# A perceiver block on one core: span attention's last steps placed in another half batch, and the order within a stretch reversed

## The chip, the cores and the metric

The kernel runs on one core of a Trainium2 chip. The metric is the device time of one execution in microseconds. Of the kernel before there are three unprofiled runs, 1526.94 us (the median), 1526.82 and 1529.74, and one profiled execution whose trace is read here.

## What is computed

Three residual blocks follow one another on `x` (32 batches x 64 positions x 256): cross attention to a context of 1601 keys per batch, "span" attention among the 64 positions, and a feed-forward part with one shared expert and 8 experts chosen by a hash of the token's position, two for each. All in float32, 16 heads of 16.

```python
x = x + cross_attention(layernorm(x), ctx, mask)        # q, k, v, softmax over 1601 keys, out
# span attention, h = layernorm(x):
span = head_reshape(h @ W_span.T, 2); value = head_reshape(h @ W_val.T, D)
mean = sigmoid(span[..., 0]) * m;     soft = softplus(span[..., 1])
diff = pos[None, None, :] - mean[..., None]
attn = softmax(-soft[..., None] * (diff * diff), axis=-1)
x = x + (attn @ value).reshape(b, m, hs) @ W_out.T
# feed-forward, xf = layernorm(x):
shared = silu(xf @ sw1 + sb1) * (xf @ sw3 + sb3) @ sw2 + sb2
x = x + (shared + sum_of_two_experts(xf) / 2) / 2
```

## The kernel before, in words

**Cross attention: 64 half batches of three stretches.** The context comes in transposed, and its 1601 keys are cut into 13 chunks of 124. A half batch `n` is a batch `b = n // 2` and one half `c` of the heads. The loop at L765 goes over the half batches, software pipelined: while the softmax of half batch `n` runs, TensorE computes the scores of `n + 1` (`psc` and `pvs`, L548), the product with the values for `n - 1` (`pvs`, L635) and the projections of the next batch's keys and values (`pk`, `pv`, L494). The softmax's maximum takes a round trip: running maxima on VectorE (`mrun`, `mx`, L589), transposes on TensorE (`pm`, L596), a reduction on VectorE (`mc`, L603), transposes back (`pb`, L611), a copy by ScalarE (`mb`, L615). Then GpSimd subtracts the maxima (L620, four instructions per half batch) and ScalarE takes the exponentials (L625). Each half batch has three stretches, numbered `3n + g`; between the cross attention's own pieces each calls `run(stretch)`, once.

**Everything else is placed by an agenda.** `agenda[stretch]` is a list of generators. `run(stretch)` advances each generator of the list up to its next `yield`; the yielded number says how many stretches later it goes on. Three kinds of generators go through it: `query_steps(t)` (the next tile's layer norm, the transposes `tr_q`, the query product `pq` and its four copies into `qbd`, L465 to L480), `finish_steps(b)` (L704: divides a batch's attention output by its sums and transposes it into `oT`) and `span_steps(t)` (L244), which holds the output product of cross attention and the whole span attention of a tile.

**A tile is two batches, so four half batches are a period.** The 16 tiles' span attentions are cut into 23 steps each, and four tables tell the stretch of each step, counted from the tile's start: `STEPS` for tiles 0 to 12, `LAST_BUT_TWO`, `LAST_BUT_ONE` and `LAST` for tiles 13, 14 and 15. Counted from zero, the steps that matter here are:

| step | what it does | lines |
|---|---|---|
| 0 | output product `po` of cross attention, residual, layer-norm statistics | L250, L253, L197-199 |
| 1, 2 | spread on GpSimd, normalisation `xn_h` on ScalarE | L205-208, L214 |
| 3 | transposes `tr_h`, copy to `hT` (ScalarE) | L221, L262 |
| 4, 5, 6 | `psp` and its copies, exponential `z`, 17 small VectorE operations | L266-305 |
| 7, 8, 9 | scores `sc` on GpSimd, ScalarE (square) and GpSimd again; `least` on VectorE | L310-318 |
| 10-13 | 16 exponentials with their sums, four per step, ScalarE | L322 |
| 14-16 | value product `pval`; reciprocal `total`; product on GpSimd | L334-348 |
| 17, 18 | transposes `psa`, copies `aT`; product `po2`, copy `o2T` | L356-372 |
| 19 | second output product `po3` (shown as `po<-woutT_sb,o2T`), residual, statistics, store of `x_kept` | L376-381 |
| 20, 21 | spread on GpSimd, normalisation `xn_f` on ScalarE | L205-214 |
| 22 | transposes `tr_f`, two copies into `xfT` (ScalarE) | L221, L389 |

In the tables a value `v` of tile `t` stands for stretch `3n + v` of half batch `n = 4t + 4`; so 24 is the first stretch of half batch `4t + 12`, 30 that of `4t + 14`. Half batches are spoken of by `n mod 4`: the "third" of a period is the one with 2.

**What sets the order.** TensorE, VectorE, ScalarE and GpSimd execute in the order in which the code issues (L731). SP, which issues the DMAs, is ordered by the tile scheduler. PSUM banks for products come from one rotating set (`mm_bank`), so an early reader of a bank can be what a later product waits for.

**The end.** After the loop, the last half batch is finished, and the stretches from 2 to 21 after it are run by L849 on. There `unit(u)` is one of 16 pieces of the shared expert (two products of `xfT` with `sw1` and `sw3`, four matmuls, `u`, L664), and `gate()` its SiLU on ScalarE (L686, L691) and product on VectorE (L687, L692). `begin` says after which stretch which units start and `gated` how many gates follow. Units 12 to 15 need the last tile's `xfT`, and after them come the experts (L900 to L941).

Of the kernel before, what the change touches and what calls it, by code (L numbers as in the profile page):

```python
# [89 lines left out]
def perceiver_kernel(ctx: ExitStack, tc: tile.TileContext, a: dict[str, bass.AP], out: bass.AP):  # L90
# [126 lines left out]
    def transposed(src, name: str):  # L217
# [10 lines left out]

    STEPS = (3, 4, 5, 6, 7, 8, 9, 11, 12, 15, 16, 17, 18, 19, 20, 20, 21, 22, 23, 24, 25, 26, 27)
    LAST_BUT_TWO = (
        3, 4, 5, 6, 7, 8, 9, 11, 12, 13, 13, 14, 15, 16, 17, 17, 17, 18, 20, 21, 22, 25, 27,
    )
    LAST_BUT_ONE = (
        2, 2, 3, 4, 5, 5, 6, 7, 8, 9, 10, 11, 12, 13, 14, 14, 14, 15, 16, 17, 17, 18, 19,
    )
    LAST = (2, 2, 3, 4, 5, 6, 8, 9, 10, 11, 12, 12, 12, 12, 13, 13, 13, 15, 16, 17, 17, 18, 19)
    SMALL = 6
# [1 line left out]
    def steps_of(t: int):  # L241
        return (STEPS, LAST_BUT_TWO, LAST_BUT_ONE, LAST)[max(0, t - NTILE + 4)]

# [339 lines left out]
    def maximum(n: int, k: int):  # L583

        dst = mrun
        if k == NKC - 1:
            dst = mxs[n] = work.tile([P, 4, P], F32, tag="mx", bufs=1, name="mx")
        dst, run = (m[:CHUNK].rearrange("p (r i) q -> p r i q", r=2) for m in (dst, mrun))
        nc.vector.tensor_tensor(dst, block_of(n, k), run, ALU.max)  # L589
# [105 lines left out]
    held_at: set = set()  # L695

    def run(stretch: int):
        for steps in agenda.pop(stretch, []):
            while (wait := next(steps, None)) == 0:
                pass  # L700
            if wait:
                agenda[stretch + wait].append(steps)
# [62 lines left out]
    for n, (b, c) in enumerate(halves[:-1]):  # L765
# [9 lines left out]
        def steps(g: int):  # L775
            run(3 * n + g)
            for u in extra.get(3 * n + g, ()):
                linear_factor(u)
# [14 lines left out]
        if not held:  # L793
            first_maxima(n + 1)
        run(3 * n)
        if n:
            values(n - 1, 1)
# [30 lines left out]
    stretch = 3 * last  # L828
# [17 lines left out]
    gate()  # L846


    begin = {4: (1, 2), 7: (7, 8, 5), 10: (9,), 12: (10,), 15: (6, 4), 19: (11,)}  # L849
    gated = {7: 2, 10: 2, 12: 1, 13: 1, 15: 1, 17: 2}  # L850
    for s in range(2, 22):
        run(stretch + s)
# [149 lines left out]
```

## Time and profile before

| | us |
|---|---|
| median of three runs (lowest, highest) | 1526.94 (1526.82, 1529.74) |
| the profiled execution | 1529.89 |
| its span, first to last instruction | 1528.1 |
| `pm` of half batch 63, where the end begins | 1362.03 |
| mean granted TensorE clock | 0.996 of full speed |

The page counts for each engine the time in which an instruction of it was under way; an engine can be busy for most of the span and still not be what the end waits for. The timeline gives groups of like instructions in the order of their start; a bracket behind a row says how long the engine had been idle before it, and what ended this. Times in the timeline are microseconds from the span's start. "PEld" is TensorE's loading of weights, which overlaps its matmuls. DMA moves 46 GB/s over the span in the mean, and the transfers of the context come ahead of their use.

### The profile page before, as it was taken

Reading aid. Unit: us, or ns where it says so; the run is one execution under the profiler, and the core shown is the slowest. Engines: PE = TensorE matmul, PEld = TensorE weight load, DVE = VectorE, ACT = ScalarE, POOL = GpSimd, SP = SyncE. Lnnn points to the kernel's source line nnn. Section 1 sums busy time; section 2 is a strip of 40 time slices with the busy share of each in tenths; the row PEclk is TensorE's granted clock in tenths of the full one; section 3 lists DMA queues with packets and bytes.
Section 4 is the critical chain, followed back from the end, with each engine's and each line's share of the span. In section 5 each row is a group of like instructions: output and inputs, shape, how many; then the busy total and the mean of one; then the engine's idle time right before and its main releaser. Section 6 shows DMA issues by size and latency. Waiting matters only on the chain.

```text
span 1528.1 us, 62953 instructions
## 1 busy us (share of the span) xinstructions
PE 1470.4 (96%) x28600; PEld 1071.4 (70%) x28600; DVE 1222.8 (80%) x2332; ACT 947.7 (62%) x1727; POOL 1119.0 (73%) x508
## 2 busy tenths in 40 slices
PE   8999999999999999999999999999999999988999
PEld 5677767777777767777776767676777767654587
DVE  4889898988889898989888898888898889873100
ACT  3565657676667657676767666675767676756411
POOL 1777787888878887879878788878788787852610
PEclk9999999999999999999999999999999999999999
DMA  5111111111111101111111111111111111004100
GB/s 173 43 38 46 46 46 46 44 45 49 49 49 50 42 23 46 53 36 49 49 50 49 50 49 32 33 45 53 36 50 49 50 46 32 6 6 159 59 28 29
DMA packets 52076, 73.82 MB, mean 48 GB/s; under 512 B 3812, under 2 KB 51040, under 8 KB 51680
## 3 DMA queue, kind: packets, MB, share of 16 engines
q1 hardware_dynamic: 50992, 69.00, 14.7%
q8 instruction: 225, 3.69, 1.0%
q10 hardware_dynamic: 816, 0.79, 0.2%
q14 instruction: 43, 0.35, 0.1%
HBM read 65.57 MB, written 4.19 MB: 46 GB/s over the span
## 4 chain that ended last, share of the span: by engine, by line
PE 72%; DVE 17%; ACT 8%; issue 2%; POOL 0%; DMA 0%; ACTq 0%; DVEq 0%; POOLq 0%
PE pv L494 18%; PE pk L494 18%; PE psc L548 11%; PE pvs L635 8%; DVE mrun L589 7%; DVE prob L572 6%; PE py L932 4%; ACT sc L322 3%; PE pm L596 2%; ACT prob L625 2%; PE u L664 2%; PE ph L914 2%; PE pb L611 2%; PE pq L465 1%; PE psa L356 1%
## 5 line engine op out<-in xcount | busy, mean ns | idle before, releaser
L620 POOL TENSOR_TENSOR prob<-prob,mb 124x1664 f32<-124x1664 f32 x252 | 937.7, 3745 | 239.4 <-ACT mb L615 231.6
L572 DVE TENSOR_TENSOR prob<-psc,madd 124x512 f32<-124x512 f32 x768 | 506.6, 680 | 70.8 <-PE psc L548 69.2
L625 ACT ACTIVATE prob<-prob 124x1664 f32<-124x1664 f32 x256 | 406.9, 1590 | 181.7 <-POOL prob L620 179.1
L589 DVE TENSOR_TENSOR mrun<-prob,mrun 124x512 f32<-124x512 f32 x704 | 486.1, 691 | 40.7 <-ACT mrun L581 28.0
L494 PE MATMUL pk<-ct,wkT_sb 128*32 128x372 f32 (+1 forms) x2512 | 387.6, 489 | 5.7 <-DMA wkT_sb<-in_wkT 5.6
L494 PE MATMUL pv<-wvT_sb,ct 128*124 128x256 f32 x3524 | 380.9, 379 | 0.4 <-DVE prob L572 0.3
L494 PEld LDWEIGHTS pv<-wvT_sb,ct 128*124 128x124 f32 x3524 | 273.6, 132 | 108.7 <-issue 14.9
L548 PE MATMUL psc<-qbd,kT 32*124 32x128 f32 x6400 | 246.6, 280 | 17.0 <-ACT hT L262 9.7
L494 PEld LDWEIGHTS pk<-ct,wkT_sb 128*32 128x32 f32 (+1 forms) x2512 | 148.9, 127 | 135.9 <-issue 88.9
L548 PEld LDWEIGHTS psc<-qbd,kT 32*124 32x124 f32 x6400 | 204.7, 182 | 54.7 <-issue 19.7
L526 ACT COPY v<-pv 124x512 f32<-124x512 f32 (+1 forms) x224 | 124.4, 556 | 164.0 <-PE pv L494 163.9
L635 PE MATMUL pvs<-prob,v 124*17 124x64 f32 x13312 | 214.3, 220 | 1.2 <-issue 1.2
L635 PEld LDWEIGHTS pvs<-prob,v 124*17 124x17 f32 x13312 | 196.7, 98 | 23.1 <-issue 15.2
L509 ACT ACTIVATE kT<-pk,cols 128x372 f32<-128x372 f32 (+2 forms) x256 | 146.7, 585 | 69.1 <-PE pk L494 69.0
L322 ACT ACTIVATE sc<-sc,least 128x64 f32<-128x64 f32 x256 | 85.7, 339 | 2.8 <-DVE least L318 2.8
L934 DVE SCALAR_TENSOR_TENSOR ot<-py,prob 128x256 f32<-128x256 f32 x16 | 6.8, 424 | 75.7 <-PE py L932 75.7
L581 ACT COPY mrun<-prob 124x512 f32<-124x512 f32 x64 | 38.2, 597 | 41.4 <-DVE soft L305 38.3
L664 PE MATMUL u<-xfT,sw_sb 128*128 128x512 f32 x128 | 61.1, 627 | 0.9 <-ACT xfT L389 0.9
L596 PE MATMUL pm<-cst,mx 124*128 124x124 f32 x256 | 42.1, 285 | 17.0 <-DVE mx L589 14.1
L611 PEld LDWEIGHTS pb<-cst,mc 128*124 128x124 f32 x256 | 29.5, 135 | 36.8 <-DVE mc L603 28.9
L548 PE MATMUL pvs<-qbd,kT 32*124 32x128 f32 x256 | 54.9, 294 | 0.0
L565 DVE TENSOR_TENSOR prob<-psc,madd_fifth 124x256 f32<-124x256 f32 x64 | 27.0, 421 | 32.2 <-PE pvs L548 31.1
(126 smaller groups left out, 1242.4 us busy)
## 6 DMA issues: line engine op xcount, KB each, us to landing
ct<-in_ctxT SPq DMA_DIRECT2D x64, 372.0 KB, 3.2
ct<-in_ctxT SPq DMA_DIRECT2D x32, 496.0 KB, 5.1
ct<-in_ctxT SPq DMA_DIRECT2D x32, 361.0 KB, 4.0
w<-in_w SPq DMA_DIRECT2D x16, 256.0 KB, 7.0
x<-in_x SPq DMA_DIRECT2D x16, 128.0 KB, 2.1
x_kept<-x SPq DMA_DIRECT2D x16, 128.0 KB, 1.8
prob<-x_kept SPq DMA_DIRECT2D x8, 256.0 KB, 5.6
out<-ot SPq DMA_DIRECT2D x16, 128.0 KB, 1.9
```

The lines of the kernel that those rows point to most:

```text
L322: nc.scalar.activation(sc[:, h, :], sc[:, h, :], AF.Exp, bias=least[:, h : h + 1], scale=-1.0, accum_out=total[:, h : h + 1],)
L494: nc.tensor.matmul(out[at:end], lhsT=lhsT[:, at:end], rhs=rhs, start=start, stop=stop, **(dict(tile_position=(0, at)) if tiled else {}),)
L509: nc.scalar.activation(kTs[c][:, k0 : k0 + kn], ps[:, :kn], AF.Identity, bias=cols[:, B_K + c : B_K + c + 1])
L526: nc.scalar.copy(vs[b % 2][:kn, 2 * u : 2 * u + n, :, :DK], ps[:kn, : n * D].rearrange("p (n h d) -> p n h d", n=n, d=DK),)
L548: product = nc.tensor.matmul(ps[:CHUNK, at * P : (at + 1) * P], lhsT=kTs[c][32 * j : 32 * j + 32, k0 : k0 + CHUNK], rhs=qbd[b // 2][32 * j ...
L572: nc.vector.tensor_tensor(pair_of(n, j)[:, c0 : c0 + 4, :].rearrange("p k (e q) -> p k e q", e=2), pss[j][:CHUNK].rearrange("p (k e q) -> ...
L589: nc.vector.tensor_tensor(dst, block_of(n, k), run, ALU.max)
L596: nc.tensor.transpose(ps[:, j * CHUNK : (j + 1) * CHUNK], m[:CHUNK, j, :], ident[:CHUNK, :CHUNK])
L620: engine.tensor_tensor(sj, sj, m[:CHUNK, j, None, :].to_broadcast([CHUNK, NKC, P]), ALU.subtract)
L625: nc.scalar.activation(pair_of(n, j), pair_of(n, j), AF.Exp)
L635: nc.tensor.matmul(pvs[32 * j : 32 * j + DK + 1, c, :, r, :], lhsT=v[:kn, k, 8 * c + h, :], rhs=pair_of(n, h // 2)[:kn, k, (h % 2) * S : ( ...
L664: nc.tensor.matmul(ps, lhsT=w[:, c, hc * P : (hc + 1) * P], rhs=xfT[:, c, :, slot], start=(c == 0), stop=(c == 1),)
```

## The change

It has four parts. In `STEPS` the last four steps go from 24 to 27 to 30 to 33, that is from the half batches with 0 and 1 (mod 4) to those with 2 and 3. In `LAST_BUT_TWO` and `LAST_BUT_ONE` late steps are taken to earlier stretches: tile 13's last four from 21, 22, 25, 27 to 21, 21, 21, 23 with the one ahead of them unchanged at 20; tile 14's sixteen exponentials are all in one stretch, and what follows them is two stretches earlier. `run` goes through its list from the back, so of the generators in a stretch the one that was put into it last is advanced first. And units 1 and 2 begin one stretch earlier. No operation is added or removed.

```diff
-    STEPS = (3, 4, 5, 6, 7, 8, 9, 11, 12, 15, 16, 17, 18, 19, 20, 20, 21, 22, 23, 24, 25, 26, 27)
+    STEPS = (3, 4, 5, 6, 7, 8, 9, 11, 12, 15, 16, 17, 18, 19, 20, 20, 21, 22, 23, 30, 31, 32, 33)
     LAST_BUT_TWO = (
-        3, 4, 5, 6, 7, 8, 9, 11, 12, 13, 13, 14, 15, 16, 17, 17, 17, 18, 20, 21, 22, 25, 27,
+        3, 4, 5, 6, 7, 8, 9, 11, 12, 13, 13, 14, 15, 16, 17, 17, 17, 18, 20, 21, 21, 21, 23,
     )
     LAST_BUT_ONE = (
-        2, 2, 3, 4, 5, 5, 6, 7, 8, 9, 10, 11, 12, 13, 14, 14, 14, 15, 16, 17, 17, 18, 19,
+        2, 2, 3, 4, 5, 5, 6, 7, 8, 9, 10, 10, 10, 10, 12, 12, 12, 13, 14, 15, 15, 16, 17,
     )
...
     def run(stretch: int):
-        for steps in agenda.pop(stretch, []):
+        for steps in reversed(agenda.pop(stretch, [])):
             while (wait := next(steps, None)) == 0:
                 pass
...
-    begin = {4: (1, 2), 7: (7, 8, 5), 10: (9,), 12: (10,), 15: (6, 4), 19: (11,)}
+    begin = {3: (1, 2), 7: (7, 8, 5), 10: (9,), 12: (10,), 15: (6, 4), 19: (11,)}
```

## The prediction

> **What bounds the kernel now.** I read the page first: engine totals, then the chain that ended last.
>
> ```profile
> span 1528.1 us, 62953 instructions
> PE 1470.4 (96%) x28600; PEld 1071.4 (70%) x28600; DVE 1222.8 (80%) x2332; ACT 947.7 (62%) x1727; POOL 1119.0 (73%) x508
> ...
> PE 72%; DVE 17%; ACT 8%; issue 2%; POOL 0%; DMA 0%; ACTq 0%; DVEq 0%; POOLq 0%
> ```
>
> TensorE has work for 1470.4 of 1528.1 us, so some 58 us of idle is all that a reordering can win. I then listed TensorE's waits (columns: engine, line waited for; total us, times, longest):
>
> ```profile
> PE pm L596 <- DVE mx L589: 14.1, 16, 2.4
> ...
> PEld psc L548 <- ACT hT L262: 11.8, 11, 1.1
> ...
> PE psc L548 <- ACT hT L262: 9.7, 11, 0.9
> ```
>
> Two waits recur about once for each of the tiles. The second is one event seen twice, by weight loads and by matmuls. To place them I cut one period (a tile, four half batches) at the pm transposes (L596) and asked for each engine's busy time per stretch: bounds and length, then PE, PEld, DVE, ACT, POOL busy with counts, the granted clock, DMA share, GB/s. The first row is half batch 8, the others 32 to 35.
>
> ```profile
> 198.43:217.69 19.26, 18.45 (x409) 13.30 (x409) 17.52 (x32) 10.82 (x14) 16.20 (x6) 1.00 0.04 13
> 704.96:725.12 20.16, 19.35 (x416) 13.93 (x413) 18.68 (x35) 12.48 (x15) 17.90 (x9) 1.00 0.06 20
> 725.12:745.48 20.36, 20.36 (x431) 14.77 (x431) 18.84 (x33) 13.33 (x28) 17.09 (x11) 1.00 0.24 70
> 745.48:768.05 22.57, 21.70 (x461) 16.48 (x457) 18.17 (x34) 18.21 (x47) 16.82 (x6) 1.00 0.06 20
> 768.05:788.64 20.59, 20.59 (x469) 15.22 (x465) 18.89 (x42) 12.58 (x18) 17.01 (x6) 1.00 0.25 71
> ```
>
> I call the four classes 0 to 3 (n mod 4). Classes 1 and 3 have no TensorE idle: what is added there is paid in full. Class 0 idles 0.81, class 2 0.87 (plus late weight loads). The timeline names both (start, length, what; in brackets the idle before it and who ended it):
>
> ```profile
> 725.12 0.64 PE L596 MATMUL pm<-cst,mx 124*128 124x124 f32 x4 [0.81 <-DVE mx L589]
> 751.91 0.82 PE L548 MATMUL psc<-qbd,kT 32*124 32x128 f32 x20 [0.87 <-ACT hT L262]
> 751.50 0.36 ACT L262 COPY hT<-tr_h 128x256 f32<-128x256 f32 x1
> 707.55 1.03 PE L376 MATMUL po<-woutT_sb,o2T 128*128 128x256 f32 x4
> ```
>
> Class 2: scores cannot start until ScalarE has copied hT out of a bank (end 751.86), and ScalarE runs without a gap from 743.34 to 752.12. The last row is po3 in class 0.
>
> **The change, part by part.** TensorE's and VectorE's instruction counts stay the same; places change.
>
> *Class 0 loses po3, the residual and statistics.* po3 starts at 707.55, the next work at 708.51: a slot of 0.96. Half batch 8 does all of this class but po3 and lasts 19.26 against 20.16: **−0.90**, with the 0.81 wait in both. So the VectorE chain that ends in mx moves with TensorE rather than standing still: it runs without a gap from 711.51 and starts on TensorE's scores. I take −0.89, for 13 tiles.
>
> *Class 1 loses tr_f (0.44) and its two copies.* Half batch 9, without tr_f, lasts 20.17 against 20.36: **−0.20**, 13 times. The reversal also puts x += po before the reduction of least; it may wait 0.2 for TensorE, and VectorE's mx is 1.06 ahead of pm there.
>
> *Class 2 gains po3 (0.87 where banks are free), residual 0.42, statistics 0.43 and 0.18.* po3 goes ahead of the values, so TensorE reaches the scores later; hT's end, which releases them, is ScalarE's and doesn't move. The scores begin 4.86 after pm (750.34), their first dozen, whose banks are free, takes some 0.4; so with po3 ahead the one that waits is reached at 4.86 + 0.87 + 0.4 = 6.1, and hT ends at 6.38. Hidden, with 0.3 to spare (issue stops before the last matmul ends, so the listed 0.87 is short of the true stall). VectorE's added 1.03 lies in its 1.57 of idle ahead of mrun. If that cover goes, po3 costs its 0.87, and the scores are late next. At stretch 1 the reversal puts pq and the qbd copies ahead of psp and z; pq's bank goes to the second pk, which comes to wait for the 1.48 of qbd: pq would end 758.93, copies 760.48, pk due 760.31: **+0.2**. Bounds: 0 (pk still later) and 1.1 (pq's whole length); I stay with the nearest row.
>
> *Class 3 gains spread, norm and tr_f with xfT following in the next class.* GpSimd idles 6.3 ahead of its next mask work there, so the 1.28 of spread is hidden; the transposes are not: **+0.22** (the mirror of class 1), 12 times; the thirteenth is in the end.
>
> *SP's queue.* The x_kept store moves with the residual, behind the first context load of the odd batch instead of the even one; the next x load behind it is wanted some three half batches later. 0; if that cover went, x's 2.1 us landing would show once per tile.
>
> *The reversal at the heavy stretch.* A generator is requeued as it ran, so a reversed list flips at every stretch. In the built order class 2, stretch 0, still has the four exponentials ahead of hT: the 0.87 stall keeps its cause. Half batches 6 and 10 meet the flip without the removal: +0.2 each.
>
> Loop: 13 × (−0.89 − 0.20) = −14.2; 12 × (0.2 + 0.22) = +5.0; half batch 62's po3, which meets no stall, +0.87; first two +0.4. Sum **−7.9 us**. Unnamed 1 to 1.9 us stalls of TensorE ("issue", eight of them) may fall differently: ±3.
>
> *The end* (pm of 63 at 1362.03, the span's end at 1528.1). Here tile 15's own chain decides:
>
> ```profile
> 1379.33 1.10 PE L250 MATMUL po<-woP_sb,oT 128*128 128x256 f32 x4 [1.59 <-DVE oT L718]
> ...
> 1385.83 0.44 PE L221 MATMUL tr_h<-cst,xn_h 128*128 128x128 f32 x2 [0.58 <-ACT xn_h L214]
> 1387.61 1.09 PE L356 MATMUL psa<-cst,sc 128*128 128x128 f32 x8 [1.34 <-POOL sc L348]
> 1388.54 0.54 PE L266 MATMUL psp<-wspanT_sb,hT 128*128 128x32 f32 x4
> ...
> 1390.02 9.98 PE L664 MATMUL u<-xfT,sw_sb 128*128 128x512 f32 x20
> 1399.84 1.03 PE L376 MATMUL po<-woutT_sb,o2T 128*128 128x256 f32 x4
> 1404.02 0.44 PE L221 MATMUL tr_f<-cst,xn_f 128*128 128x128 f32 x2 [3.15 <-ACT xn_f L214]
> ```
>
> In the changed order tile 14's psa stands ahead of tile 15's po in TensorE's queue; psa waits for tile 14's exponentials, total and GpSimd's 1.90 product. These stay where they are (psa about 1387.5 against 1387.61), so po(15) goes from 1379.33 to 1388.4: +9.1. Behind it: x at 1389.5 (1380.47), xn_h +6.8, psp 1394.8 (1388.54), units 7, 8, 5 from 1395.35, +5.3. Tile 15's small VectorE work follows +5.9. Part is absorbed: before, ScalarE was held by table load and gates until the square at
>
> ```profile
> 1407.39 1.05 ACT L314 ACTIVATE sc<-sc 128x1024 f32<-128x1024 f32 x1
> ```
>
> and after it is free; the square starts 1411.4, +4.0. From there the chain (mult, least, exponentials, product, psa, po3, tr_f, last units, experts) is the same as before. So +4.0, and up to +5.5. Bounds: +9.1 (nothing absorbed) and −3 (the 3.15 wait for xn_f goes and nothing takes its place).
>
> *Two rules of the Trainium skill.* "TensorE: Matmul & The Clock Gate", section "Part 1: The HAM clock gate", speaks against: about 3.4 us of little work halves TensorE's clock, for about 3.4 us. In this trace the granted clock was 0.50 from 1388.9 to 1392.3, after waits of 0.58 and 1.34, and four matmuls of a unit took 2.96 instead of 1.72. In the changed end TensorE would idle about 4 us ahead of psa(15). By the rule that is an additional 1.7 us, by the row 1.24. As before has one such window already and the phase is unknown, I count 0.3: end **+4.3**. "ScalarE: Activation LUTs", "What ACT_TABLE_LOAD costs", gives 2.66 us per switch with its drain. The change orders the exponentials together and saves two of eight loads in the end: −5.3 by the rule. The trace has 1.28 for one (1376.86 to 1378.14, with the instruction before it ending at 1376.84: no drain), so −2.6, and the chain passes by TensorE and VectorE there: counted 0.
>
> Sum: −7.9 + 4.3 = **−3.6**. The profiled run took 1529.89 (span 1528.1), so 1526.3 on its terms; it lies 2.95 above the median 1526.94, from which the forecast is **1523.4**.
>
> **Rivals.** A measurement here tells 0.2%, 3.05 us, from no change.
> - *Slower: po3 isn't hidden in class 2.* The hT copy, or the bank before it, moves with TensorE, so the stall comes after po3 in its full length. For: in class 0 a chain did move with TensorE, the spare is only 0.3, and VectorE's mrun or a bank may come late instead. Against: what ScalarE's run up to hT takes from TensorE (pb, tr_h) is queued ahead of po3. Price 12 × 0.87 = 10.4: 1533.8. From 0.56 per period up the kernel is slower by over 0.2%.
> - *The end doesn't slip*: units fill psa's wait, xn_f's 3.15 goes. −7.9 − 3: 1516.0. Against: po(15) really stands behind psa(14).
> - *The class 0 wait grows by what po3 frees* (mx doesn't move): loop −7.9 + about 4, the end +4.3: 1527.3. Half batch 8 speaks against it.
>
> **Chances.** Forecast 0.48 (its own range 1520.5 to 1526.5: ±3 of issue stalls; 0.30 of it under 1523.9, 0.18 within 0.2%); slower rival 0.24; end that doesn't slip 0.18; cancelled 0.10. Faster 0.48, same 0.28, slower 0.24. The range 1516 to 1532 leaves out about half of either outer rival, some 0.2.
>
> **What would show it.** Right: class 0 near 19.3, class 1 near 20.15, class 2 near 22.75 with hT's stall no longer among the waits, class 3 near 20.8; po(15) 27 us after pm of half batch 63 instead of 17; six table loads in the end. Wrong: class 2 above 23.2; pm waiting over 1.5 in class 0; or units 7, 8, 5 starting within 2 us of their former place.

## The result: slower, though undisturbed half batches came out as worked

The changed kernel takes 1537.37 us (median of four runs, 1535.69 to 1538.26) against 1527.78 us (four runs, 1526.82 to 1529.74): the ratio is 1.006, with a 95% interval of 1.0042 to 1.0077. The profiled execution took 1537.91 us. Its page gives these totals:

```profile
span 1535.9 us, 62938 instructions
...
PE 1476.5 (96%) x28600; PEld 1072.8 (70%) x28600; DVE 1223.3 (80%) x2332; ACT 944.7 (62%) x1725; POOL 1119.9 (73%) x508
```

TensorE has as many instructions as before (28600 matmuls) but is busy for 6.1 us more: the same instructions took longer. The page alone does not say where. The same cut as in the prediction, at the pm transposes, for half batches 48 to 51 (bounds and length, then busy time of PE, PEld, DVE, ACT, POOL with counts, granted clock, DMA share, GB/s):

```profile
1042.53:1061.82 19.29, 18.48 (x409) 13.33 (x409) 16.56 (x30) 10.42 (x13) 15.71 (x5) 1.00 0.01 4
1061.82:1081.96 20.14, 20.14 (x429) 14.43 (x429) 18.85 (x33) 13.05 (x24) 16.86 (x11) 1.00 0.23 64
1081.96:1104.67 22.71, 22.38 (x465) 17.01 (x461) 19.07 (x37) 18.32 (x48) 17.71 (x9) 1.00 0.08 26
1104.67:1125.48 20.81, 20.81 (x471) 15.44 (x467) 18.89 (x42) 13.62 (x21) 17.23 (x6) 1.00 0.27 81
```

These are the lengths that recur in each class: 19.29, 20.14, 22.71 and 20.81 us. The forecast had 19.3, 20.15, 22.75 and 20.8. Per period that is some 0.73 us less than before, over the twelve periods from half batch 12 to 59 8.7 us. But not every half batch has its class's length: in class 3 only three of the twelve do, and their mean is 21.68 us (before: seven of twelve at 20.59, mean 21.02). Besides, pm of half batch 63 stands at 1361.06, a mere 0.97 us earlier than before (1362.03). From there to the end of the span it takes 174.80 us instead of 166.08. So two places have to be explained: nearly 10 us that the loop gave back, and 8.7 us lost in the end.

**The loop: half batches that are longer than their class.** TensorE's waits (engine, line waited for; total us, times, longest) have this row in the kernel before:

```profile
PE psc L548 <- issue: 5.6, 8, 1.6
```

And these in the changed kernel:

```profile
PE pm L596 <- DVE mx L589: 14.3, 17, 2.4
PE psc L548 <- issue: 8.4, 11, 1.6
...
PE psc L548 <- ACT hT L262: 2.7, 11, 0.9
```

The hT wait has fallen from 9.7 to 2.7 us, though it still occurs 11 times where the forecast had it gone; mx's is what it was. The row between them is the one to look at: "issue" means that TensorE waited for nothing that the profile shows. Half batch 19 has the longest, here in TensorE's timeline (start, length, what; in brackets the idle time before it):

```profile
446.17 0.81 PE L548 MATMUL psc<-qbd,kT 32*124 32x128 f32 x17
448.58 0.71 PE L548 MATMUL psc<-qbd,kT 32*124 32x128 f32 x15 [1.60 <-issue]
449.22 0.64 PE L596 MATMUL pm<-cst,mx 124*128 124x124 f32 x4
449.70 3.10 PE L494 MATMUL pk<-ct,wkT_sb 128*128 128x496 f32 x4
```

The scores stop in the middle of a group of 32 like matmuls. The DMA view of 443 to 449.5 us (queue, packets, MB, share of 16 engines) shows what else went on:

```profile
q1 hardware_dynamic: 816, 1.26, 62.5%
q8 instruction: 1, 0.02, 0.8%
```

Three pieces of context fill the DMA engines, and one packet of instructions goes in their midst. The trace's packet records put this packet at 446.18 to 447.06; TensorE resumes at 448.58, 1.5 us after. Of the unnamed stalls of over 0.6 us in half batches 12 to 59 of both kernels, each one resumes 1.2 to 1.6 us after such a packet has ended. TensorE's instructions themselves place the stalls further. Counting the matmuls and weight loads in the trace, before's six such stalls come after 12411, 17502, 21064, 36843, 38624 and 42187 of them, with 48, 68, 82, 144, 151 and 165 packets fetched: 254.4 to 254.6 instructions for each packet between neighbours. The changed kernel's nine give 254.4 to 254.8. So these stalls all lie at the same place, the end of a fetched block. A second thing is in the last row above: four pk matmuls took 3.10 us where they take 1.83 elsewhere. The granted clock says why (same columns as above):

```profile
450.10:453.50 3.40, 3.40 (x8) 1.55 (x6) 2.24 (x4) 0.66 (x1) 0.00 (x0) 0.50 0.00 0
453.50:456.90 3.40, 3.40 (x147) 2.97 (x147) 1.70 (x3) 2.08 (x4) 2.49 (x1) 0.99 0.02 5
```

After the stall the clock was 0.50 for 3.4 us, and half batch 20 became 1.69 us longer than its class. Adding up what half batches 12 to 59 are longer than the recurring length of their class gives 8.2 us in the kernel before and 17.9 in the changed one. I call this sum "stalls" below; in half batch 20 it includes the slow clock. Of it, 5.1 us before and 10.4 in the changed kernel lie in class 3, 2.0 and 5.8 in class 0.

**The end.** TensorE's timeline of the changed kernel from the last half batch on (tile 14's psa, then po(15), the po of tile 15; the last four rows are tile 15's psa, po2 and po3 and the last tr_f):

```profile
1382.73 1.98 PE L664 MATMUL u<-xfT,sw_sb 128*128 128x512 f32 x4 [2.20 <-ACT prob L691]
1386.32 1.09 PE L356 MATMUL psa<-cst,sc 128*128 128x128 f32 x8 [1.61 <-POOL sc L348]
1387.25 1.03 PE L250 MATMUL po<-woP_sb,oT 128*128 128x256 f32 x4
...
1391.69 1.61 PE L376 MATMUL po<-woutT_sb,o2T 128*128 128x256 f32 x4 [2.82 <-ACT o2T L372]
1393.09 0.63 PE L221 MATMUL tr_h<-cst,xn_h 128*128 128x128 f32 x2
1394.19 1.06 PE L266 MATMUL psp<-wspanT_sb,hT 128*128 128x32 f32 x4 [0.46 <-ACT hT L262]
1395.06 10.79 PE L664 MATMUL u<-xfT,sw_sb 128*128 128x512 f32 x20
...
1423.83 1.97 PE L356 MATMUL psa<-cst,sc 128*128 128x128 f32 x8 [3.63 <-POOL sc L348]
1425.73 1.40 PE L366 MATMUL po<-aT,vbd 128*32 128x64 f32 x32
1427.91 2.08 PE L376 MATMUL po<-woutT_sb,o2T 128*128 128x256 f32 x4 [0.79 <-ACT o2T L372]
...
1434.90 0.38 PE L221 MATMUL tr_f<-cst,xn_f 128*128 128x128 f32 x2
```

Of these last rows, the kernel before has:

```profile
1419.50 1.09 PE L356 MATMUL psa<-cst,sc 128*128 128x128 f32 x8 [1.05 <-POOL sc L348]
...
1422.76 1.13 PE L376 MATMUL po<-woutT_sb,o2T 128*128 128x256 f32 x4 [1.01 <-ACT o2T L372]
...
1427.16 0.38 PE L221 MATMUL tr_f<-cst,xn_f 128*128 128x128 f32 x2
```

po(15) starts 26.2 us after pm of 63 (17.3 before), psp 33.1 (26.5), the square (step 8) of tile 15 50.7 (45.4). At psa(15) the kernel is 5.3 us behind, and from there on the same instructions are slower: psa 1.97 instead of 1.09, po3 2.08 instead of 1.13. The clock over two stretches:

```profile
1392.20:1399.00 6.80, 6.34 (x14) 3.50 (x13) 2.70 (x7) 2.10 (x4) 1.03 (x3) 0.50 0.54 173
1422.90:1433.10 10.20, 8.39 (x48) 5.26 (x49) 3.07 (x6) 4.38 (x8) 2.57 (x6) 0.50 0.04 13
```

That is 17.0 us at half clock, where the kernel before has 6.8, in two windows (both have another 6.8 where the end begins):

```profile
1388.90:1392.30 3.40, 3.40 (x37) 2.07 (x37) 0.38 (x2) 2.59 (x4) 0.00 (x0) 0.50 1.10 349
1406.00:1409.40 3.40, 3.40 (x6) 1.29 (x5) 1.78 (x3) 3.39 (x6) 0.88 (x1) 0.50 0.02 5
```

When the last transposes tr_f are reached, the 5.3 us have become 8.7.

### The profile page after: what moved, and what is told of

It reads as the page before. It is cut to its first block, busy times and chain, and to the rows that moved or that the text cites. A ratio compares the mean times of both kernels' runs of the same rounds, so it can differ in the third digit from the quotient of the medians.

```text
span 1535.9 us, 62938 instructions
## 1 busy us (share of the span) xinstructions
PE 1476.5 (96%) x28600; PEld 1072.8 (70%) x28600; DVE 1223.3 (80%) x2332; ACT 944.7 (62%) x1725; POOL 1119.9 (73%) x508
## 4 chain that ended last, share of the span: by engine, by line
PE 70%; DVE 17%; ACT 8%; issue 2%; POOL 1%; DMA 1%; POOLq 0%; DVEq 0%; SPq 0%; ACTq 0%
PE pk L494 18%; PE pv L494 18%; PE psc L548 10%; PE pvs L635 9%; DVE mrun L589 7%; DVE prob L572 6%; PE py L932 4%; PE u L664 2%; ACT sc L322 2%; PE pm L596 2%; ACT prob L625 2%; PE ph L914 2%; PE pb L611 2%; ACT qbd L473 1%; PE pq L465 1%
## 5 line engine op out<-in xcount | busy, mean ns | idle before, releaser
L596 PE MATMUL pm<-cst,mx 124*128 124x124 f32 x256 | 41.5, 283 | 15.5 <-DVE mx L589 14.3
```

The lines of the kernel that those rows point to most:

```text
L596: nc.tensor.transpose(ps[:, j * CHUNK : (j + 1) * CHUNK], m[:CHUNK, j, :], ident[:CHUNK, :CHUNK])
```

## The experiments

The "end" in the table is from pm of half batch 63 to the end of the span; it, pm and the stalls come from the one profiled execution of each run, the ratio from the timed runs against the kernel before on the same chip. The runs are spread over several chips.

| run | ratio (95% interval) | pm of 63 | stalls | end |
|---|---|---|---|---|
| before | | 1362.0 | 8.2 | 166.1 |
| changed | 1.006 (1.0042-1.0077) | 1361.1 | 17.9 | 174.8 |
| before, no loads | 0.9964 (0.9952-0.9976) | 1357.7 | 4.9 | 166.2 |
| changed, no loads | 0.999 (0.9981-0.9999) | 1352.3 | 9.3 | 174.6 |
| end tables alone | 0.9995 (0.9986-1.0005) | 1365.0 | 11.1 | 163.6 |
| STEPS alone | 0.9951 (0.9935-0.9968) | 1355.3 | 13.4 | 165.9 |
| reversal alone | 1.0025 (1.0016-1.0034) | 1365.7 | 11.0 | 167.5 |
| STEPS and reversal | 1.0003 (0.9992-1.0013) | 1365.3 | 21.2 | 168.3 |
| all but the reversal | 0.9937 (0.9917-0.9957) | 1354.7 | 11.8 | 162.5 |
| all, reversal in the loop only | 0.9995 (0.9987-1.0003) | 1362.7 | 18.7 | 164.2 |

### Without context loads

Theory A: the stalls are instruction fetches behind context transfers. In `load_context`:

```diff
-        for g in range(len(GROUPS)):
-            load_piece(b, g)
+        cts[b] = cts[0]
```

> The kernel before, with every batch reading the context tiles of batch 0, so that no context is loaded after the start (the output is that of batch 0's context). Theory A (late instruction fetches: TensorE's unnamed stalls in the loop are fetches of its instructions queued behind a context transfer): the stalls outside the named waits go, so half batches 12 to 59 all sit at their class's length (20.16, 20.35, 22.57, 20.59) and pm of half batch 63 comes about 8.5 us earlier, near 1353.5; span near 1519.5. Theory B (the stalls come from the order of the work itself, a bank or an engine): the stalls of 0.5 to 1.9 us stay at half batches 15, 19, 24, 30, 43, 47 and the span stays within 2 us.

> The changed kernel with the same omission of context loads after the start. Theory A: its 17.9 us of stalls in half batches 12 to 59 go, all sit at 19.29, 20.14, 22.71, 20.81, and pm of half batch 63 comes near 1343.5, about 9.5 to 10 us ahead of the kernel before without loads; the end stays some 9 us longer than before's, so the two spans without loads are equal within 2 us. Theory B: the stalls stay where they are, pm of 63 near 1361.

Half of theory A holds. Without the loads the stalls fall from 8.2 to 4.9 and from 17.9 to 9.3 us, so the transfers do lengthen them; but they do not vanish. What remains resumes 1.2 to 1.6 us after an instruction packet as well: in half batch 23 of the changed kernel without loads, a stall of 1.24 us ended at 516.00, with the packet at 513.37 to 514.65 and no context on the queue. So the fetch is late by itself at times. Theory B, under which nothing would change, falls too. The end is unmoved by the loads (166.2 and 174.6 us): its loss has another cause. The two spans were expected to be equal within 2 us and are 1523.9 and 1526.9: the changed order kept 4.4 us more of stalls.

### The parts of the change, one by one

Each of these takes over the lines of the diff for the part that is named, and leaves the others as before.

> Only the two end tables and begin changed; STEPS and the order within a stretch as before. Theory (the end's loss comes from the reversal meeting the new tables, psa(14) ahead of po(15)): po(15) stays ahead of psa(14), some 17 us after pm of 63, and the end is between -3 and +3 us of before's 166.07. Rival (the tables alone make the end late): the end is +6 us or more. Loop as before, pm of 63 at 1362 with up to 5 us of fetch stalls dealt otherwise.

> Only STEPS changed, the order within a stretch and the end as before. Classes 0 to 3 at 19.28, 20.14, 22.57 (po3 hidden in the hT wait, no wait of pk for qbd since pq stays behind psp) and 20.81: twelve periods are 10.4 us shorter than before's. Theory C (the added stalls come with the moved steps: without po3 and with tr_f the fast stretches of class 0 and 3 outrun the fetch of instructions): stalls of 16 to 21 us in half batches 12 to 59 against before's 8 to 11, so the loop is only 0 to 3 us shorter than before's. Theory D (they come with the reversal): stalls of 8 to 11 us, pm of 63 near 1352 to 1354. The end 166 to 167.

> Only the reversal. Classes 20.16, 20.35, 22.72 (pk waits 0.15 for qbd), 20.59: twelve periods 1.8 us longer than before's. Theory C: stalls of 8 to 11 us as before, pm of 63 near 1364 to 1367. Theory D: stalls of 16 us or more, pm of 63 near 1372. The end 166 to 168.5.

> STEPS and the reversal as changed; the end tables and begin as before. The loop's classes are those of the changed kernel (19.29, 20.14, 22.71, 20.81). The end is +0 to +2 us of before's 166.07, since po(15) isn't behind psa(14). Theory A: the stalls depend on how TensorE's instructions lie in the fetched blocks, which is the same as in the changed kernel up to the end, so the loop ends near 1361 as there, and the span is 1527 to 1529. Rival (the stalls are run to run noise): the loop ends anywhere from 1352 to 1362.

The tables alone do not hurt: their end is 2.5 us shorter than before's (within the range given), although po(15) starts 24.2 us after pm and not at 17. **STEPS alone makes the kernel faster, by 0.5%**, with the classes as expected; here are 2 and 3 of its profile, same columns:

```profile
1078.00:1100.62 22.62, 22.44 (x465) 17.13 (x461) 19.19 (x37) 18.28 (x47) 17.74 (x9) 1.00 0.07 24
1100.62:1121.42 20.80, 20.80 (x470) 15.43 (x466) 18.89 (x42) 13.58 (x21) 17.23 (x6) 1.00 0.26 80
```

Class 2 takes in po3, residual and statistics at 22.58 to 22.62 us, against 22.57 without them. The stalls of STEPS alone are 13.4 us, between what the theories C (16 to 21) and D (8 to 11) said. The reversal alone costs 0.25%: 1.7 us for pk's wait in class 2, an end 1.4 us longer, and stalls of 11.0 us. Neither part has the whole excess by itself; both together have 21.2. In that run the loop ended at 1365.3, outside of what I expected, in a profiled execution at the slow edge of its own runs (1527.63 to 1537.29). Stalls of one profile are thus good to a few us.

### Without the reversal, and without it in the end only

```diff
-        for steps in reversed(agenda.pop(stretch, [])):
+        for steps in agenda.pop(stretch, []):
```

> The changed kernel without the reversal: STEPS, both end tables and begin as changed. If the parts add up (STEPS alone -7.3 us, the end tables alone an end of 163.6 instead of 166.1): loop as in the run of STEPS alone (pm of 63 at 1354 to 1357), end 163 to 165, time 1518 to 1520, some 9 to 10 us below before. If the end tables need the reversal: the end is above 168 and the time 1525 or more.

For the other, the list is reversed only in stretches ahead of the last half batch:

```diff
-        for steps in reversed(agenda.pop(stretch, [])):
+        due = agenda.pop(stretch, [])
+        for steps in reversed(due) if stretch < 3 * (2 * B - 1) else due:
```

> The changed kernel with the reversal up to half batch 62 only; the last stretches run in the order put. Theory (the end's loss is the reversal meeting the new tables, psa(14) ahead of po(15)): loop as in the changed kernel, pm of 63 at 1360 to 1362; po(15) 16 to 18 us after it instead of 26, one half-clock window of 10.2 us fewer, end 163 to 167 instead of 174.8, time 1525 to 1530. Rival (the end's loss comes from the state in which the loop leaves off): end 172 or more.

**All but the reversal has the lowest time of these forms**, 0.63% below before (1521.05 us against 1529.43, where 1518 to 1520 was expected); its interval overlaps that of STEPS alone. By the profiles, the reversal in the end costs 10.6 us (174.8 against 164.2), the reversal in the loop 8.1 (pm of 63 at 1362.7 against 1354.7).

The time in the end came out as expected, but not by the step that I had given: po(15) starts 24.8 us after pm of 63, not 16 to 18, against 26.2 with the reversal. With po(15) ahead of psa(14) it comes a mere 1.4 us earlier; both stand behind unit 2, which waits for a gate on ScalarE, and on ScalarE the gate stands behind tile 14's sixteen exponentials, which the new table has put into one stretch. A late po(15) does not make the end late by itself either: with the end tables alone it comes at 24.2 us, and that end is shorter than before's. ScalarE's timeline, with the rows of VectorE and GpSimd that wait for it, shows what decides. The changed kernel:

```profile
1406.11 0.43 ACT L389 COPY xfT<-tr_f 128x128 f32<-128x128 f32 x2 [8.61 <-PE tr_f L221]
1406.56 1.28 ACT L280 ACT_TABLE_LOAD   x1
1407.85 0.23 ACT L280 ACTIVATE z<-z 128x32 f32<-128x32 f32 x1
...
1408.12 0.20 DVE L293 TENSOR_TENSOR mrun<-z,one_two 128x32 f32<-128x32 f32 x1 [9.87 <-ACT z L280]
...
1409.78 1.90 POOL L310 TENSOR_TENSOR sc<-cst,mean 128x1024 f32<-128x1024 f32 x1 [14.04 <-DVE at L300]
...
1411.71 1.06 ACT L314 ACTIVATE sc<-sc 128x1024 f32<-128x1024 f32 x1 [1.05 <-POOL sc L310]
```

And with the reversal in the loop only:

```profile
1398.20 1.28 ACT L280 ACT_TABLE_LOAD   x1
1399.49 0.23 ACT L280 ACTIVATE z<-z 128x32 f32<-128x32 f32 x1
1403.26 0.43 ACT L389 COPY xfT<-tr_f 128x128 f32<-128x128 f32 x2 [3.54 <-PE tr_f L221]
...
1406.16 1.05 ACT L314 ACTIVATE sc<-sc 128x1024 f32<-128x1024 f32 x1
```

Reversed, tile 14's xfT copies stand ahead of tile 15's z on ScalarE. They wait for tr_f(14), which is behind units 7, 8 and 5 on TensorE; so z, 32 elements wide, stands behind a wait of 8.61 us, and the small operations (waiting 9.87 us for z), the scores on GpSimd (waiting 14.04 for them), the square and the sixteen exponentials of tile 15 behind it. Relative to pm of 63, z is at 46.8 us with the reversal and at 36.8 without, the square at 50.7 and at 43.4.

### Where the instruction blocks end

Is the excess of stalls an accident of where 16 KB blocks of instructions end? Blocks of that size are what the Trainium skill states ("Runtime: NRT & Kernel Launch", section "Instruction fetch mechanics": 256 instructions each), and the trace agrees: 225 packets for 3.69 MB. The page adds that the fetch is hidden behind the issue of instructions. Here it isn't always: 104 value matmuls with their 104 weight loads go in 1.65 us, so a block can be used up in about 2, while one packet takes 0.9 us or more and TensorE resumes 1.2 to 1.6 us after its end.

A first attempt put 128 empty instructions ahead of TensorE's first product.

> The kernel before with 128 empty instructions ahead of TensorE's first matmul, where it waits for the first load anyway: every later TensorE instruction lies half a fetched block (16 KB[...]) further on. Nothing else moves. Theory E (the stalls depend on where a block ends within a half batch): classes unchanged at 20.16, 20.35, 22.57, 20.59, but the stalls appear at other half batches, and their sum of 8.4 us changes by 3 us or more. Rival (stalls follow from the order of the work or from the loads, whatever the block): the same half batches 15, 19, 24, 30, 43, 47 and 8 to 11 us in sum.

> The changed kernel with the same 128 empty instructions. Classes unchanged at 19.29, 20.14, 22.71, 20.81. Theory E: the stalls lie in other half batches than 19, 20, 24, 27, 28, 31, 35, 43, 47, and their sum of 17.9 us may fall to 8 to 12. Theory C: the half batches are others, but the sum stays at 15 to 21 us, since class 0 and 3 outrun the fetch wherever a block ends. The end stays at 174 to 175.

The profiles have 62953 and 62938 instructions, as many as without: the empty instructions were not in the program. These two are repetitions of before (ratio 1.0003, stalls 7.0) and of the changed kernel (1.0056, stalls 15.5), which tells how well a sum repeats, and nothing of theory E. The next ones use real matmuls:

```diff
+    for _ in range(64):
+        nc.tensor.matmul(spare_pvs[:32, :32], lhsT=zero, rhs=zero, start=True, stop=True)
     queries = query_steps(0)
```

> The kernel before with 64 small matmuls (32x32, zeros, into a bank that is written over afterwards) ahead of TensorE's first product: 64 weight loads and 64 matmuls, 128 instructions, half a fetched block of 256. They cost up to 4 us at the start, which is seen from pm of half batch 12 and taken off. Theory E (stalls depend on where a block ends): from half batch 12 to 59 the stalls leave 19, 24, 43, 47 for others, the classes stay; their sum is anywhere from 3 to 20 us. Rival: the same half batches and 7 to 11 us.

> The changed kernel with the same 64 matmuls. Theory E: the stalls leave half batches 19, 20, 27, 31, 35, 43, 47 for others; if their sum falls to 8 to 12 us the 17.9 us were an accident of block ends, if it stays at 15 to 21 the changed order has more of them wherever the blocks end. End 174 to 175 as in the changed kernel.

The trace has 128 more matmuls and 128 more weight loads, two of each for one in float32: a whole block of 256, one packet more (226), and the stalls in the same half batches (19, 24, 43, 47 before). Theory E says just this for a whole block, so it is a control. With 32 it is half a block:

> The kernel before with 32 small matmuls ahead; in float32 each became two weight loads and two matmuls in the trace, so this is 128 instructions, half a block (the 64 of the former run were a whole block: one packet more, 226, and the stalls in the same half batches). Theory E: the stalls leave half batches 19, 24, 43, 47 for others; classes unchanged (20.16, 20.35, 22.57, 20.59); sum 3 to 20 us. Rival (the place in the work decides, not the block's end): the same half batches, 7 to 9 us.

> The changed kernel with 32 small matmuls, half a block. Theory E: the stalls leave 19, 27, 31, 35, 43, 47; the sum is 8 to 14 us and the loop some 4 to 9 us shorter. Theory C (the order outruns the fetch wherever blocks end): others, but 15 to 21 us in sum. End 174 to 175 either way.

> The version without the reversal, with 32 small matmuls. Theory E: its 10.4 us of stalls go to other half batches and the sum changes by 3 us or more either way. If the version's gain is sound and not a lucky lie of the blocks, it stays below before by 4 us or more: 1517 to 1526.

| | no shift | whole block | half a block |
|---|---|---|---|
| before: largest stalls in half batches | 19, 24, 43, 47 | 19, 24, 43, 47 | 31, 35, 36, 59 |
| before: sum | 8.2 | 8.6 | 9.8 |
| changed: sum | 17.9 | 17.7 | 16.2 |
| without reversal: sum | 11.8 | not run | 12.0 |
| before: ratio, end | 1, 166.1 | 1.0006, 164.6 | 0.9983, 169.2 |
| changed: ratio, end | 1.006, 174.8 | 1.0052, 173.8 | 1.0019, 172.0 |
| without reversal: ratio, end | 0.9937, 162.5 | not run | 0.9916, 164.6 |

Theory E is right about the place and wrong about the sum. Half a block moves the stalls to other half batches, a whole one doesn't: the stalls do depend on where a block ends, and, with the counts above, that they are late fetches is shown. But the sums stay: the changed order has 16 to 18 us at both phases, before 8 to 10, the form without the reversal 12. So of theory C it holds that the order brings them, not luck. A third phase, a quarter of a block, gave no result. The counts also say why a shift could hardly change a sum: a tile has 3524 of these instructions, 13.85 blocks, so the block ends wander through the period and are back after about seven tiles (19 and 47 are 28 half batches apart), and each run meets nearly every phase.

At half a block the changed kernel is slower than before by 0.36% (1.0019 to 0.9983) rather than 0.6, and the expected end of 174 to 175 us was missed: 172.0, where before has 169.2. The clock makes most of this difference in the end. From tile 15's psa to the last tr_f the kernel before takes 7.66 us in five of the six profiles with its order, without half clock; at half a block it has 6.8 us of half clock there and takes 9.86. The six profiles with the changed order have 3.4 to 9.3 us of it and take 8.49 to 11.07. The form without the reversal keeps its gain (ratio 0.9916, 0.9899 to 0.9932).

### The load of x

In class 3, where most of the stalls sit, the order on TensorE is the same with and without the reversal (read row by row in half batch 39). What differs is, among other things, the load of the next x, which with the reversal goes out 0.2 us into class 3 and without it 0.7 us ahead of class 3. One more buffer should have taken it from there:

```diff
-        xs[t] = work.tile([P, D], F32, tag="x", bufs=5, name=f"x{t}")
+        xs[t] = work.tile([P, D], F32, tag="x", bufs=6, name=f"x{t}")
```

> The changed kernel with six instead of five buffers for x, so that the load of the next tile's x need not wait for xn_f to have read the oldest one, and goes out in class 2 behind the x_kept store instead of 0.2 us into class 3. Theory F (with the reversal this load lands 1.2 to 2.3 us into class 3, just where TensorE's next instruction packet is due, and delays it): class 3's stalls fall from 10 to 12 us to 5 to 8, the sum from 17.9 to 10 to 13, the loop by 4 to 7 us. Rival (the load has no part in it): class 3 stays at 10 to 12. Classes and end (174 to 175) as in the changed kernel.

> The version without the reversal with six buffers for x. There the load goes out 21.9 us into class 2 and lands within the first microsecond of class 3. Theory F: class 3's stalls of 7.1 us fall by 0 to 3, the time by 0 to 3 us: 1517 to 1521. Rival: no change, or a new collision of x with the x_kept store in class 2: class 2 grows.

> The kernel before with six buffers for x, for comparison: its x load goes out in class 1, where the stalls are 0.0. Both theories: stalls stay at 7 to 10 us, pm of 63 at 1360 to 1363, time within 2 us of before.

Inconclusive: the load stayed where it was (its packets at 1.0 to 1.7 us of half batch 27 as without the buffer), so theory F was not put to the test. Stalls were 15.9, 15.3 and 7.3 us, ratios 1.0045 (1.0027 to 1.0063), 0.9952 (0.9935 to 0.9969) and 0.9991 (0.9982 to 1.0001).

The packet records of the runs above decide more. They give the start of the same four packets, in us after the pm of their half batch; in half batch 59 there is no load of x, since the last tile's has come before:

| packet, in half batch | 93, 27 | 107, 31 | 190, 55 | 204, 59 |
|---|---|---|---|---|
| STEPS alone | 0.60 | 1.23 | 1.00 | 1.69 |
| all but the reversal | 0.88 | 1.22 | 0.93 | 1.50 |
| STEPS and reversal | 2.85 | 3.19 | 2.64 | 3.58 |
| changed | 2.87 | 3.22 | 2.63 | 3.41 |

With the reversal each goes out 1.6 to 2.3 us later, with the load of x and without it, so that load is not needed for the delay. These four half batches have their class's length without the reversal and are together 3.7 us longer in the changed kernel. That is most of what the reversal adds to the moved steps: 17.9 against 11.8 us here, and in the mean 17.6 us (seven profiles with both) against 13.1 (four with the moved steps alone). Why the same packet goes out later in the reversed order stays open.

## Why the prediction was wrong

- **Classes 0 and 1, right** where no late fetch falls into them. -0.87 and -0.21 came for -0.89 and -0.20; the mx wait stayed at 0.81.
- **Class 2, right.** po3 was hidden in the hT wait (shown by STEPS alone at 22.6 us), and qbd cost 0.13 for 0.2. The slower rival's mechanism did not occur; the kernel is slower for other reasons.
- **Class 3, right** for the recurring length, +0.22 (20.81). In the mean over its twelve half batches it is +0.66, and the rest is the next point.
- **The step that failed in the loop** is the term "Unnamed 1 to 1.9 us stalls [...] may fall differently: ±3". I took them as dealt at random and centred on no change. They rose by 9.7 us (1.69 of it slow clock behind one of them), and that repeats: 15.5 to 17.7 in four further profiles with the whole change, 7.0 to 9.8 in four of before. They are TensorE's own instructions coming late, which the prediction has at nothing. The moved steps add to them (13.1 in the mean of four profiles), and the reversal on top of the moved steps adds more (17.6 in the mean of seven). The removed and hidden work (po3 ahead of the values, the hT wait) was slow work between stretches of 208 instructions in 1.65 us. That it gave the fetch its time is my reading, not shown; shown are the late packets, that the stalls lie at block ends and grow with the loads, that the sum follows the order, and that with the reversal packets of class 3 go out some 2 us later.
- **The step that failed in the end** is the clock term, "As before has one such window already and the phase is unknown, I count 0.3". From psa(15) on, half clock cost another 3.4 us in the profiled pair. The rule of the Trainium skill that the prediction names ("TensorE: Matmul & The Clock Gate", section "Part 1: The HAM clock gate": an idle window of about 3.4 us halves the clock, a busy one as long restores it), from which it had worked out 1.7 us and then set it aside, was nearer, and still short: here the clock stayed low for 10.2 us, in which TensorE was busy for 8.39. The phase did count, as luck: with half a block ahead the changed kernel lost 0.8 us there and the one before 2.2.
- **The order's own cost in the end** was "+4.0, and up to +5.5" at the square; 5.3 came, part of it already slow clock. The size was about right and the reason not. po(15) came late by about the forecast 9.1 us (8.9), but chiefly for unit 2 and its gate; standing behind psa(14) is 1.4 us of it. And not po(15) set the square: z did, behind the xfT copies on ScalarE, a place in a queue that the prediction does not name.
- **The sum:** -8.7 in the steady classes, -1.8 in the rest of the loop (where -0.2 had been worked out for half batches 60 to 62 and +0.4 for the early ones), stalls +9.7, end +8.7: +7.9, where the profiled pair differs by +8.0 (7.7 by the spans) and the forecast had -3.6.

## What to carry to other kernels

Where an engine issues thousands of short instructions, cutting the slow work between them may only uncover the fetch of the instructions: before counting such a gain, look at the "issue" waits and the instruction packets beside them. To test whether such stalls are fetches, count the instructions between them. Measure the parts of a combined change apart; here one part was worth 0.5%, and another, added to it, cost more than that. When the order in a list decides two engines' queues, follow the smallest instruction on the critical chain through every queue: a 0.23 us exponential queued behind two copies came 10 us later here (46.8 against 36.8 us after pm).

## What was not expected of the hardware

TensorE's clock fell to 0.50 not just in the end: one late fetch of 1.6 us was followed by 3.4 us at half clock, 1.69 us lost on top of the stall, though the stall is less than half of the idle stretch that the rule above names. All windows of half clock in these traces last 3.4, 6.8 or 10.2 us, the one cut off by the end of a run aside, and they lie on a grid: in the changed kernel they begin at 450.12, 1361.48, 1392.20 and 1422.92 us, which is 267, 9 and 9 times 3.41 us apart, in the one before at 1361.61, 1388.92 and 1405.99, 8 and 5 times. So what a wait costs in clock can depend on where in the grid it falls, as the two ends at half a block suggest. And a float32 matmul of 32x32 counts as two weight loads and two matmuls.
